# Cross attention and a mixture of experts on one core: contexts of batches 0 and 1 projected first, empty rows stored expert by expert, a last tile in chunks, a plan in pieces

## The chip, the cores and the metric

The kernel runs on one core of one Trainium2 chip. All data are float32. A core has a matrix engine (TensorE, PE in the profile, with its weight loads PEld), VectorE (DVE), ScalarE (ACT), GpSimd (POOL), SyncE (SP, used here only to issue transfers) and 16 DMA engines. Each engine runs its own list of instructions in order and waits for the others by semaphores. The metric is the device time in microseconds (us) from start to end of one execution; smaller is better.

## The reference

`x` and `ctx` are 8 batches of 256 rows of 512 numbers. First attention: the rows of x, normalised, are queries in 32 heads of 16; the rows of the context are keys and values in 8 groups that 4 heads share. Then a mixture of experts: every row goes through a shared network (704 wide) and through two of eight experts (352 wide), chosen from two of four groups.

```python
h = layernorm(x)
score = einsum(h @ Wq.T, ctx @ Wk.T) / 4           # per head; keys of a group for 4 heads
x = x + softmax(score) @ (ctx @ Wv.T) @ Wfc.T + bfc
h = layernorm(x)
scores = softmax(h @ gate_weight.T)                 # 8 experts, 4 groups of 2
w, i = group_limited_topk(scores)                   # 2 groups, in them 2 experts
routed = sum_n w_n * (silu(h @ gate_n.T) * (h @ up_n.T)) @ down_n.T
shared = (silu(h @ sh_gate.T) * (h @ sh_up.T)) @ sh_down.T
return x + routed + shared
```

On the host, weights are only permuted.

## The kernel before, in words

**Attention** (`attention`, from line 539). A batch is 8 units; a unit is 8 (head, half of the queries) pairs, one PSUM tile of 128 x 2048 scores. The steps of a unit:

- `maxima` (L810, L819): 16 matmuls put the scores with queries on the partitions into the tile `s`; DVE reduces it to the row maxima `nm` (2.29 us).
- `place` (L827 to L833): the maxima are transposed and written into a 17th row of the queries `qT`, so that the next product subtracts them.
- `weights` (L843, L851): 8 matmuls of 17 x 512 give the transposed scores less their maxima, in the same PSUM region as `maxima`; ACT takes exponentials (`ex`, 1.88 us).
- `values` (L862) multiplies `ex` by the values, and `divide` scales.

There is one region of PSUM for scores (`ps_s`, 8 KB a partition). The maxima of a later unit and the exponentials of an earlier one alternate in it, so PE does other work in between: the queries, keys and values of later batches (`project`, L713 to L795), the output projection of an earlier batch (`close`, L890), its router (L942) and its shared expert (`Shared.pieces`, L172 to L203).

**The planner.** Each of these works is a generator that emits a few instructions and then yields `(cost, open, rest)`: the PE time just emitted, whether a PSUM tile is still open (others then do not cut in), and for how much PE work the next piece should be put off, because another engine has to finish first. Costs are estimates in us. `Others.fill(now, least, most, warm)` emits pieces between two steps of attention, choosing the work furthest behind its due time; where nothing is ready, it calls `warm()`, which is two 128 x 128 matmuls of the identity that nobody reads. `finish(s)` emits pieces until `s` is done. With this the order on PE, ACT, DVE and SP is fixed when the kernel is built. POOL's order is left to the framework, which places POOL's instructions itself.

**Norms.** `normed(b)` takes mean and variance of batch b's rows on DVE, the reciprocal deviation on POOL (`pow`, L682), and centres the rows on DVE (L686).

**Start of the program.** SP loads batch 0's rows and context (L642 to L647), then `wq`, then batch 1's rows and context; ACT issues `wkv`. After 8 `warm` calls come batch 0's norm, then `project(0)`: keys and values (L720, L731), their copies (L741, L742), transposed rows (`tx`, L694, copies `xT`), queries (`pq`, L776), and the transfer of the queries into bands (`qT`, L791). `put` moves the keys into bands by DMA (L749). `copy` goes to ACT or DVE as `copy.free` says.

**Transfers among the attention.** `transfers()` (L1203) is a generator that is advanced once per step of attention: `wfc`, `bfc`, the router's and the shared expert's weights, then zeros to the rows behind the experts' tables, then one transfer (L1216) that writes zeros to the first 128 rows of each of the eight experts' tables in `rows`: 2112 KB from an `empty` tile of 264 KB.

**Closing a batch.** `close(b)` loads the batch's rows of x again as residual (`acc`, 2 transfers of 256 KB on SP), POOL adds the bias (L894), PE makes 4 + 4 matmuls `fc` per half (L901), DVE adds (L910), and the second norm follows.

**Routing.** `router(b)` computes gates and positions; GpSimd scatters the normalised rows to `rows` (L1026). After the last batch `plan` (L1034 to L1120) computes on DVE which tile of 128 rows belongs to which expert, from counts: about 30 small operations of up to 0.85 us each. Its yields have `rest` 0 and are "free", so the planner emits them one after another. The last batch's shared expert is left over and runs beside what follows; its products `act` (L185, L186) are DVE's too.

**Experts** (`routed`, L341 to L536). 35 tiles of up to 128 rows run: 8 first ones (one per expert), 24 full ones, 3 that two experts share. Per tile: load `xs` (L377), turn it (`rx`, `rxT`, L388 to L390), 8 matmuls of 128 x 352 for gate and up (`rg`, L421), silu on ACT (L429), product on DVE (`ract`, L431), three transposes (`ra`, `raT`, L437 to L440), 3 (or 6, with two experts' halves) matmuls `ro` (L449), scaling by the routing weight on DVE (`ry`, L457), and an indirect transfer by POOL that adds the rows to the result in memory (`y<-ry`, L460). The order of a step is: turn the next tile, `up` of this one, `down` of the one before, `turn_act` of this one. The added rows of one tile wait for those of the tile before, since both may write the same row. All weights `wgu_all`, `wd_all` stay in SBUF and are loaded on SP, the first ones while attention ends. A second run under a condition (L525) was not executed.

Of the kernel before, what the change touches and what calls it, by code (L numbers as in the profile page):

```python
# [340 lines left out]
def routed(ctx, tc, ps_m, wgu, wd, ident, rows, t_exp, t_row, t_one, t_all, t_end, blank, out, tail, right):  # L341
# [69 lines left out]

    def up(i):
        e = exps[i] = i if i < N_EXP else value(t_exp, i - N_EXP, ENG.PE, N_EXP - 1)
        gu = [ps_g.tile([P, F], F32, tag=f"g{k}", name=f"rg{i}_{k}") for k in range(2)]
        xT = xTs.pop(i)
        for k in range(2):
            for c in range(NC):
                f = slice(k * F, (k + 1) * F)
                w = wgu_all[:, bass.ds(e, 1), c, f].rearrange("p o f -> p (o f)")
                for part, w in halves(i, w, wgu_2[:, c, f]):  # L420
                    nc.tensor.matmul(  # L421
                        gu[k][part],
                        lhsT=xT[:, c, part],
                        rhs=w,
                        start=(c == 0),
                        stop=(c == NC - 1),
                    )
        sg = work.tile([P, F], F32, tag="sg", name=f"rsg{i}")
        nc.scalar.activation(sg, gu[0], AF.Silu)  # L429
        acts[i] = work.tile([P, F], F32, tag="act", name=f"ract{i}")  # L430
        nc.vector.tensor_mul(acts[i], gu[1], sg)  # L431
# [10 lines left out]
    def down(i):  # L442
        e = exps.pop(i)
        o = ps_y.tile([P, D], F32, tag="y", name=f"ro{i}")
        aT = aTs.pop(i)
        for fc, (_, fn) in enumerate(FCH):
            w = wd_all[:fn, bass.ds(e, 1), fc].rearrange("p o d -> p (o d)")
            for part, w in halves(i, w, wd_2[:fn, fc]):
                nc.tensor.matmul(  # L449
                    o[part],  # L450
                    lhsT=aT[:fn, fc, part],
                    rhs=w,
                    start=(fc == 0),
                    stop=(fc == len(FCH) - 1),
                )
        y = work.tile([P, D], F32, tag="y", bufs=3, name=f"ry{i}")
        nc.vector.tensor_scalar(y, o, w1s.pop(i), None, ALU.mult)  # L457

        for to, (part, _) in zip(ids.pop(i), halves(i, None, None)):
            nc.gpsimd.indirect_dma_start(  # L460
                out=out,
                out_offset=bass.IndirectOffsetOnAxis(ap=to, axis=0),
                in_=y[part],
                in_offset=None,
                compute_op=ALU.add,
            )

# [28 lines left out]
    def run(tiles):  # L496
# [3 lines left out]
        for n, i in enumerate([*tiles, None]):  # L500
            if 3 <= n + 2 < len(tiles):
                load(tiles[n + 2])
            if i is not None and i + 3 < N_EXP:
                up_weights(i + 3)
                down_weights(i + 3)
            for k, at in zip(halfs, seconds):
                if at == n:
                    second(tiles[k])
            if n + 1 < len(tiles):
                turn(tiles[n + 1])  # L510
            if i is not None:
                up(i)
            if n > 0:
                down(tiles[n - 1])
            if i is not None:
                turn_act(i)
# [22 lines left out]
def attention(  # L539
# [102 lines left out]
    def load_batch(b):  # L642

        xt = load_tiles(None if b == 1 else p2, b, "x", 1)
        cT = p2.tile([P, NC, S], F32, tag="cT", name=f"cT{b}")
        nc.sync.dma_start(cT, ctxT[b])
        return xt, cT  # L647

    loaded = {0: load_batch(0)}
    wkv_sb = cp.tile([P, NC, 2 * KVH * HD], F32, name="wkv_sb")  # L650
    nc.scalar.dma_start(wkv_sb, wkv)
    wq_sb = cp.tile([P, NC, D], F32, name="wq_sb")
    nc.sync.dma_start(wq_sb, wq)
    loaded[1] = load_batch(1)
# [45 lines left out]
    def normed(b):  # L700

        yield 0, False, 3.0 if b > 2 else 0, True
        xt, _ = loaded[b]
# [9 lines left out]
    def project(b):  # L713

        xt, cT = loaded.pop(b)
# [3 lines left out]
        for c in range(NC):  # L719
# [7 lines left out]
            if c % 2:  # L727
                yield 0.88, True, 0
        for kc in range(QC):
# [8 lines left out]
            if kc == 0:  # L738
                yield 0.88, True, 0
        k = p1.tile([P, S], F32, tag="k", name=f"k{b}")  # L740
# [5 lines left out]
        def put(G, dma):  # L746
# [4 lines left out]
        put(0, nc.sync)  # L751
        if b > 0:
            put(1, nc.sync)
        yield 0.88, False, 0

        xT = p1.tile([P, NC, S], F32, tag="xT", name=f"xT{b}")
# [3 lines left out]
        if b == 0:  # L760
            put(1, nc.scalar)

        nxt = b + 1 if b > 0 else 2
        if nxt < B and nxt not in loaded and b != 1:
            loaded[nxt] = load_batch(nxt)
# [268 lines left out]
    def plan():  # L1034
# [4 lines left out]
        yield 0, False, 0, True  # L1039
# [24 lines left out]
        yield 0, False, 0, True  # L1064
# [17 lines left out]
        yield 0, False, 0, True  # L1082
# [6 lines left out]
        for name, sl, start, end, base in (  # L1089
# [13 lines left out]
            yield 0, False, 0, True  # L1103
            nc.vector.tensor_mul(here, one, base.unsqueeze(1).to_broadcast(shape))
            nc.vector.tensor_reduce(row[:, sl], here, AX.X, ALU.add)

# [15 lines left out]
    PROJECT = 12 * 0.88 + 2 * 0.44  # L1122
    CLOSE = 2 * (0.44 + 4 * 0.88)
# [20 lines left out]
    for _ in range(8):  # L1144
        warm()
# [7 lines left out]
    projected = [others.add(project(0), PROJECT, 0, 1, norms[0])]  # L1153
    others.finish(projected[0])
    gates = {}
    for b in range(1, B):
        start = -LAG if b < DEEP else UNITS * b - 5.5 * LAG
        projected.append(
            others.add(project(b), PROJECT, start, UNITS * b - 1.5 * LAG, projected[-1], norms[b])
# [43 lines left out]
    def transfers():  # L1203
# [10 lines left out]
        yield  # L1214

        nc.sync.dma_start(  # L1216
            rows[: N_EXP * S_R].rearrange("(e s) w -> s e w", s=S_R)[:P],
            empty.unsqueeze(1).to_broadcast([P, N_EXP, W]),
        )

    loads = transfers()
    others.fill(-LAG, 2.0, 2.0, warm)
# [104 lines left out]
```

## Time and profile before

Three runs took 961.0, 955.32 and 957.47 us, median 957.47. The profiled execution itself took 959.21; its span is 957.4.

| stage | from to (us) | length | PE busy | DVE busy | clock |
|---|---|---|---|---|---|
| loading | 0 to 5 | 5.0 | 3.2 | 1.2 | 1.00 |
| attention, batch 0 | 5 to 100 | 95.0 | 93.0 | 48.8 | 1.00 |
| closing of batch 0 | 100 to 121 | 21.0 | 17.8 | 15.5 | 0.84 |
| attention up to batch 3's shared expert | 121 to 480 | 359.0 | 355.1 | 221.9 | 1.00 |
| the rest of attention | 480 to 620 | 140.0 | 139.8 | 76.2 | 1.00 |
| last router, plan | 620 to 655 | 35.0 | 33.1 | 18.8 | 1.00 |
| experts | 655 to 930 | 275.0 | 274.3 | 69.6 | 1.00 |
| last tile and end | 930 to 957.4 | 27.4 | 10.4 | 3.5 | 0.75 |

"Busy" is the time in which an engine has an instruction under way; length less busy is idle. The clock is the share of full speed that was granted to TensorE. The profile also tells, for every wait, which engine and instruction ended it; it follows the chain of work from the last instruction back; and it counts transfers by queue. Arrows such as `nm<-s` mean output from input; `x16` counts instructions.

### The profile page before, as it was taken

What the parts mean: (1) busy time and instruction counts of PE and PEld (TensorE: products, weight loads), DVE (VectorE), ACT (ScalarE), POOL (GpSimd) and SP (SyncE); (2) the same over time, 40 slices, a digit from 0 to 9 for tenths busy, and PEclk for the clock granted to TensorE, in tenths of its full rate; (3) what the DMA queues carried; (4) which work ended last, traced back from release to release, by engine and by line L of the source; (5) the groups of instructions that cost most, each with busy time, mean ns of one, the idle gap of its engine ahead of it and who ended that gap; (6) DMA issues with size and microseconds to landing.
All of it is one profiled execution on the core that took longest, in us unless ns stands there. A gap on an engine that the chain in (4) does not pass through costs nothing.

```text
span 957.4 us, 12926 instructions
## 1 busy us (share of the span) xinstructions
PE 926.7 (97%) x4989; PEld 545.7 (57%) x4989; DVE 455.5 (48%) x1026; ACT 202.9 (21%) x256; POOL 134.0 (14%) x171
## 2 busy tenths in 40 slices
PE   8999899999999999999999999999999999999992
PEld 8765466455545554664654645675666565565661
DVE  3653756656666755654775645361222222222221
ACT  1223033223223222222232231101111111111110
POOL 4000100211101101010121021120111121211211
PEclk9999899999999999999999999999999999999997
DMA  6368310120111111011111011089953443533322
GB/s 219 92 176 275 93 51 2 58 55 29 46 56 34 47 22 47 5 48 35 34 47 45 1 47 45 32 303 371 398 118 67 108 120 67 152 75 64 55 32 32
DMA packets 37790, 86.22 MB, mean 90 GB/s; under 512 B 6176, under 2 KB 14624, under 8 KB 35808
## 3 DMA queue, kind: packets, MB, share of 16 engines
q1 hardware_dynamic: 29040, 66.43, 21.5%
q0 software_dynamic: 7648, 17.83, 8.8%
q10 hardware_dynamic: 1040, 1.12, 0.4%
q8 instruction: 42, 0.69, 0.3%
q14 instruction: 20, 0.16, 0.1%
HBM read 54.99 MB, written 25.93 MB: 85 GB/s over the span
## 4 chain that ended last, share of the span: by engine, by line
PE 84%; DMA 4%; DVE 4%; SPq 3%; issue 1%; ACT 1%; POOL 1%; ACTq 0%; POOLq 0%; DVEq 0%
PE rg L421 17%; PE gu L172 14%; PE ro L449 9%; PE o L192 9%; PE s L843 6%; PE s L810 6%; PE fc L901 5%; PE av L862 5%; PE pq L776 4%; PE rx L388 2%; DMA rows<-empty 1%; DVE nm L819 1%; PE ra L437 1%; SPq L749 1%; SPq L791 1%
## 5 line engine op out<-in xcount | busy, mean ns | idle before, releaser
L819 DVE TENSOR_REDUCE nm<-s 128x8 f32<-128x2048 f32 x64 | 146.5, 2288 | 75.4 <-PE s L810 73.2
L421 PE MATMUL rg<-wgu_all,rxT 128*128 (+2 forms) x560 | 171.6, 459 | 0.0
L172 PE MATMUL gu<-hT,gu_w 128*128 128x256 f32 x704 | 167.1, 386 | 2.6 <-DVE act L186 1.9
L851 ACT ACTIVATE ex<-s 128x2048 f32<-128x2048 f32 x64 | 120.2, 1878 | 226.6 <-PE s L843 215.1
L172 PEld LDWEIGHTS gu<-hT,gu_w 128*128 128x128 f32 x704 | 128.9, 190 | 43.9 <-issue 24.1
L421 PEld LDWEIGHTS rg<-wgu_all,rxT 128*128 128x128 f32 (+1 forms) x560 | 101.1, 186 | 54.3 <-issue 6.9
L449 PE MATMUL ro<-wd_all,raT 128*128 (+5 forms) x210 | 96.5, 595 | 0.8 <-DVE raT L439 0.8
L460 POOL DMA_INDIRECT y<-ry,rid x38 | 58.4, 1537 | 254.5 <-DVE ry L457 197.5
L192 PE MATMUL o<-down,act 128*128 128x512 f32 x192 | 90.1, 604 | 0.3 <-DVE q L333 0.3
L431 DVE TENSOR_TENSOR ract<-rg,rsg 128x352 f32<-128x352 f32 x35 | 18.4, 525 | 141.1 <-PE rg L421 141.1
L810 PE MATMUL s<-kT,qT 16*128 16x256 f32 x1024 | 75.0, 404 | 3.5 <-DVE nm L819 3.3
L843 PE MATMUL s<-qT,kT 17*128 17x512 f32 x512 | 73.0, 640 | 2.9 <-DVE nm L819 2.2
L810 PEld LDWEIGHTS s<-kT,qT 16*128 16x128 f32 x1024 | 47.3, 186 | 34.4 <-ACT ex L851 14.9
L449 PEld LDWEIGHTS ro<-wd_all,raT 128*128 128x128 f32 (+3 forms) x210 | 38.4, 186 | 44.2 <-issue 37.1
L901 PE MATMUL fc<-wfc_sb,o 128*128 128x512 f32 x128 | 61.9, 610 | 0.1
L776 PE MATMUL pq<-xT,wq_sb 128*128 128x256 f32 x256 | 60.9, 385 | 0.8 <-ACT xT L333 0.8
L862 PE MATMUL av<-ex,v 128*32 128x512 f32 x512 | 61.5, 598 | 0.0
L1026 POOL DMA_INDIRECT rows<-lnf,idx x32 | 31.7, 991 | 209.5 <-DVE idx L1020 147.8
L457 DVE TENSOR_SCALAR ry<-ro,rw 128x512 f32<-128x512 f32 x35 | 26.3, 751 | 71.2 <-PE ro L449 71.2
L390 ACT COPY rxT<-rx 128x512 f32<-128x512 f32 x35 | 20.5, 586 | 185.0 <-PE rx L388 185.0
L192 PEld LDWEIGHTS o<-down,act 128*128 128x128 f32 x192 | 34.0, 190 | 41.5 <-issue 40.3
L776 PEld LDWEIGHTS pq<-xT,wq_sb 128*128 128x128 f32 x256 | 46.8, 190 | 14.1 <-issue 7.3
(176 smaller groups left out, 719.8 us busy)
## 6 DMA issues: line engine op xcount, KB each, us to landing
wgu_all<-wgu SPq DMA_DIRECT2D x8, 1408.0 KB
xs<-rows SPq DMA_DIRECT2D x32, 264.0 KB
wd_all<-wd SPq DMA_DIRECT2D x8, 768.0 KB
wgu<-wgu SPq DMA_DIRECT2D x3, 1408.0 KB
cT<-ctxT SPq DMA_DIRECT2D x8, 512.0 KB
acc<-x SPq DMA_DIRECT2D x16, 256.0 KB
y<-acc SPq DMA_DIRECT2D x16, 256.0 KB
x<-x SPq DMA_DIRECT2D x14, 256.0 KB
```

Of the source, the lines that this page charges most:

```text
L172: nc.tensor.matmul(ps[:, i], lhsT=self.gu[k][:, c, i * P : (i + 1) * P], rhs=hT[:, c], start=(c == 0), stop=(c == NC - 1),)
L192: nc.tensor.matmul(ps, lhsT=act[:, k, q * P : (q + 1) * P], rhs=self.down[:, k], start=(i == 0), stop=(i == len(SCH) - 1),)
L421: nc.tensor.matmul(gu[k][part], lhsT=xT[:, c, part], rhs=w, start=(c == 0), stop=(c == NC - 1),)
L449: nc.tensor.matmul(o[part], lhsT=aT[:fn, fc, part], rhs=w, start=(fc == 0), stop=(fc == len(FCH) - 1),)
L460: nc.gpsimd.indirect_dma_start(out=out, out_offset=bass.IndirectOffsetOnAxis(ap=to, axis=0), in_=y[part], in_offset=None, compute_op=ALU.add,)
L776: nc.tensor.matmul(ps[:, i], lhsT=wq_sb[:, c, part], rhs=xT[:, c], start=(c == 0), stop=(c == NC - 1),)
L810: nc.tensor.matmul(ps[:, r, j], lhsT=qT[band, G, j0 + j, qc * P : (qc + 1) * P], rhs=kT[band, G], start=True, stop=True,)
L819: nc.vector.tensor_reduce(nms[b, G, j0][:, qc], ps, AX.X, ALU.max, negate=True)
L843: nc.tensor.matmul(ps[:, r], lhsT=kT[band, G, kc * P : (kc + 1) * P], rhs=qT[band, G, j0 : j0 + 2], start=True, stop=True,)
L851: nc.scalar.activation(ex, ps, AF.Exp, scale=HD**-0.5)
L862: nc.tensor.matmul(av[32 * r : 32 * r + 32], lhsT=vs[b % DEEP][:, kc, 4 * G + r], rhs=ex[:, r], start=(kc == 0), stop=(kc == QC - 1),)
L901: nc.tensor.matmul(ps, lhsT=o[:, c, qc * P : (qc + 1) * P], rhs=wfc_sb[:, c], start=(c == 0), stop=(c == NC - 1),)
```

## The change

It has four parts.

1. **Contexts first.** A batch's load is divided in `load_context` and `load_rows`. SP now issues: context 0, rows 0, context 1, `wq`, rows 1. `project` gives its key and value part to a new generator `keys(b)`. At the start there are 5 `warm` calls instead of 8 (there are 17 in the whole program before and after); then `keys(0)`, the first norm, the first two pieces of `keys(1)`, and only then the rest of `project(0)`. The remainder of `keys(1)` is emitted where the planner wants it. For later batches `keys(b)` stands at the head of `project(b)`. Batch 1's copy of the keys gets another buffer, and the copies during the first `fill` go to DVE instead of ACT.
2. **Empty rows expert by expert.** The one transfer of 2112 KB becomes eight of 264 KB, one per step of attention.
3. **Plan in pieces.** The plan's yields ask for a `rest` of 1.7 instead of 0, and one yield is added, so that pieces of the last shared expert come between.
4. **Last tile in chunks.** `run` calls `last(i, before)` for the last tile: gate product, silu, `down` of the tile before, and then the up product in three chunks of 128, 128 and 96 columns, each followed by its product on DVE, its transpose and its `down` matmuls as soon as they can go. The matmuls of other tiles are the same, in new functions `product`, `down_chunk`, `add_up`.

Since the planner decides from costs and rests, parts 1 to 3 also shift the order of other pieces. On PE the order between batch 0 and 480 us differs by small swaps; from batch 3's shared expert to the last tile it is the same. On SP, the `acc` loads of batch 0 stand behind the query transfers of batch 4 in the new order; before they stood ahead of six pieces of them. On POOL, batch 5's deviation stands ahead of batch 0's bias adds in the new order, and behind them before.

```diff
+    def last(i, before):
+        of_expert(i)
+        g = ps_g.tile([P, F], F32, tag="g0", name=f"rg{i}_0")
+        product(g, i, slice(0, F))
+        sg = work.tile([P, F], F32, tag="sg", name=f"rsg{i}")
+        nc.scalar.activation(sg, g, AF.Silu)
+        down(before)
...
+        def values_of(fc):
+            f0, fn = FCH[fc]
+            u = ps_g.tile([P, F], F32, tag=f"g{int(fc < 2)}", name=f"ru{i}_{fc}")[:, :fn]
+            product(u, i, slice(F + f0, F + f0 + fn))
+            nc.vector.tensor_mul(a[:, f0 : f0 + fn], u, sg[:, f0 : f0 + fn])
+
+        def turned(fc):
+            f0, fn = FCH[fc]
+            ps = ps_m.tile([P, P], F32, tag="m", name=f"ra{i}_{fc}")
+            nc.tensor.transpose(ps[:fn], a[:, f0 : f0 + fn], ident)
+            nc.vector.tensor_copy(aTs[i][:fn, fc], ps[:fn])
+
+        values_of(0)
+        values_of(1)
+        turned(0)
+        values_of(2)
+        turned(1)
+        down_chunk(o, i, 0, FCH[0][1])
+        turned(2)
+        for fc in (1, 2):
+            down_chunk(o, i, fc, FCH[fc][1])
+        del xTs[i]
+        add_up(o, i)
...
-    loaded = {0: load_batch(0)}
+    contexts = {0: load_context(0)}
     wkv_sb = cp.tile([P, NC, 2 * KVH * HD], F32, name="wkv_sb")
     nc.scalar.dma_start(wkv_sb, wkv)
+    loaded = {0: load_rows(0)}
+    contexts[1] = load_context(1)
     wq_sb = cp.tile([P, NC, D], F32, name="wq_sb")
     nc.sync.dma_start(wq_sb, wq)
-    loaded[1] = load_batch(1)
+    loaded[1] = load_rows(1)
...
+    def project(b):
+        if b > 1:
+            yield from keys(b)
+        xt = loaded.pop(b)
...
         nxt = b + 1 if b > 0 else 2
         if nxt < B and nxt not in loaded and b != 1:
-            loaded[nxt] = load_batch(nxt)
+            contexts[nxt] = load_context(nxt)
+            loaded[nxt] = load_rows(nxt)
...
-        yield 0, False, 0, True
+        yield 0, False, 1.7, True
...
-    for _ in range(8):
+    for _ in range(5):
         warm()
...
-    projected = [others.add(project(0), PROJECT, 0, 1, norms[0])]
+    others.finish(others.add(keys(0), PROJECT_KEYS, 0, 1))
+    others.finish(norms[0])
+    of_keys = others.add(keys(1), PROJECT_KEYS, 0, 1)
+    for _ in range(2):
+        others.step(of_keys)
+    projected = [others.add(project(0), PROJECT - PROJECT_KEYS, 0, 1, norms[0])]
     others.finish(projected[0])
...
-        yield
-
-        nc.sync.dma_start(
-            rows[: N_EXP * S_R].rearrange("(e s) w -> s e w", s=S_R)[:P],
-            empty.unsqueeze(1).to_broadcast([P, N_EXP, W]),
-        )
+
+        for e in range(N_EXP):
+            yield
+            nc.sync.dma_start(rows[e * S_R : e * S_R + P, :], empty)
 
     loads = transfers()
+    copy.free = "DVE"
     others.fill(-LAG, 2.0, 2.0, warm)
```

## The prediction

> **What bounds the kernel now.** First the page: busy time and the granted clock by slices.
>
> ```profile
> PE 926.7 (97%) x4989; PEld 545.7 (57%) x4989; DVE 455.5 (48%) x1026; ACT 202.9 (21%) x256; POOL 134.0 (14%) x171
> PEclk9999899999999999999999999999999999999997
> ```
>
> TensorE (PE) carries the program. Both kernels issue the same matmuls, 17 `warm` calls included, apart from the split of one tile. So I count the time as PE work plus PE's idle time plus what a lowered clock costs, and ask which idle goes and which comes. Second view: stages, cut where the clock changes (columns: stretch, length, busy of PE, PEld, DVE, ACT and POOL, clock, DMA share, GB/s).
>
> ```profile
> 5.00:114.00 109.00, 103.98 (x711) 72.34 (x710) 60.29 (x86) 24.60 (x30) 11.02 (x23) 1.00 0.60 179
> 114.22:121.05 6.83, 6.83 (x27) 4.34 (x28) 3.93 (x5) 0.36 (x1) 0.57 (x1) 0.50 0.00 1
> 121.05:620.00 498.95, 494.89 (x3038) 275.78 (x3037) 298.06 (x608) 136.34 (x147) 53.11 (x79) 1.00 0.12 37
> 620.00:655.00 35.00, 33.09 (x128) 23.20 (x127) 18.84 (x86) 2.88 (x7) 6.78 (x7) 1.00 0.83 315
> 930.00:957.40 27.40, 10.43 (x31) 5.24 (x29) 3.47 (x8) 0.46 (x1) 4.65 (x3) 0.75 0.24 30
> ```
>
> Idle of PE: 5.02 us up to 114, 4.06 in 499 us of attention, 1.91 in the stage of the last router and the plan, 17 at the end. In the second row the clock is halved for 6.83 us, which costs 6.83 x 0.5 = 3.41. Third, who PE waited for (total, times, longest):
>
> ```profile
> PE s L810 <- DVE nm L819: 3.3, 2, 3.1
> PE gu L172 <- DVE act L186: 1.9, 1, 1.9
> PE ro L449 <- DVE raT L439: 0.8, 1, 0.8
> PE pq L776 <- ACT xT L333: 0.8, 1, 0.8
> PE s L843 <- ACT ex L851: 0.6, 1, 0.6
> ```
>
> Fourth, the chain of waits through the longest of these, and at the end (start, length, what).
>
> ```profile
> 100.34 5.45 DMA acc<-x
> 105.85 1.26 POOL acc L894
> 107.47 1.26 POOL acc L894
> 108.73 0.67 POOL rstda L682
> 109.43 1.00 DVE x L686 x2
> 111.97 2.19 DVE nm L819
> 114.20 2.09 PE s L810 x16
> ...
> 937.29 0.76 DVE ry L457
> 938.32 4.97 DMA y<-ry,rid
> ```
>
> Batch 0's residual rows arrive late, POOL adds the bias in its order, batch 5's norm stands behind it on POOL, and VectorE (DVE), in order, holds the row maxima of a score tile until 109.43. PE idles 3.11 us and then runs at half clock. At the end the last scatter waits until the one before has landed.
>
> **Part 1, contexts first.** The counts are unchanged; three `warm` calls move from the start into the attention. One call is 4 recorded matmuls, at full clock 2.15 / 19 = 0.113 us each (the timeline of the `warm` tile after 5.0 us), so 1.36 us leave and return; interleaved pairs of calls in the timeline take 1.06 to 1.20 instead of 0.90, so the return may cost 0.2 more. I take 0. Idle that can go: 0.14 before the first key matmul (7.30), 0.84 before the queries (12.76), and the first score group, 1.81 us instead of the 1.08 of the next, held by the query transfer (0.73): 1.71. Now x, key weights and context (1.5 MB) are in front of the first matmul; afterwards 1 MB. At the 436 GB/s of 5.0 to 7.2 us that is 1.2 us sooner, so keys start near 6.0; five `warm` calls end at 1.81 + 16 x 0.212 + 4 x 0.113 = 5.7. Keys 3.6, half of batch 1's keys 1.8, transposes 0.9 and 1.0 more of batch 1 fill PE until 13.3, when the copies of x (two of 0.60) are just done. New: the second score group waits for DVE, which now first copies batch 1's keys, values and x (0.42 + 0.41 + 2 x 0.65) and centres batch 2's x (1.0): about 0.4 idle. Sum -1.3; bounds -1.7 and, if the query transfer lands as late as it did relative to its copies, 0.
>
> **Part 2, empty rows expert by expert, and the order around batch 0's close.** Before, one 2112 KB store is issued at 77.51; the chain follows it for 14.26 us, the eight query issues behind it take 9.55 us against 5.60 for another eight, and SyncE (SP) reaches the residual loads at 100.34. Afterwards a 264 KB store is issued at a time, and in the new POOL order batch 5's norm stands ahead of the bias adds. That unties DVE from them. But SP's new order puts the residual loads behind the eight query transfers of batch 4 and one chunk: about 98.9 (queries copied) + 8 x 0.64 + 0.6 = 104.6 on my count of PE, later than before. Queued behind them: a chunk, batch 5's key bands, batch 6's loads, first needed 10 us on. The first load took 5.45 us with 1 MB of other loads ahead; with one chunk (14.26 / 8 = 1.8 us) and small pieces ahead I take 4: landing 108.7, bias add done 110.0. DVE wants it after the maxima of the fourth group, near 110.4. So no wait, with 0.4 to spare. The statistics of batch 5's x before the second group's maxima cost PE 0.9. Idle 3.11 becomes 0.9 and the halved clock (3.41) goes: -5.6. The 0.61 at 87.8 and 0.18 at 99.2 are gone in the new order by the same count, exponentials being 1.88 and the work between them over 2: -0.7. Bounds: -7.3 (no idle left), and from the other side the load 5.8 us later in SP's order (nine issues of 0.64), all of it PE idle beyond the old 3.11: +5.8.
>
> Here a rule of the skill speaks against the change. The Trainium skill, "DMA: Bandwidth & Descriptors", section Bandwidth / Measured, says to batch transfers to at least 1 MiB, and gives about 2.0 us fixed plus bytes at 436 GB/s for each (section Anatomy of one DMA). An estimate by that page: a chunk in front costs 2.6 us instead of 1.8, the residual is 0.4 late, and the total below is 11.1 instead of 11.5. No row of this profile has such a chunk.
>
> **The stretch between, 121 to 480.** PE's order differs by small swaps, and is the same from batch 3's shared part on. The 4.06 us of idle there are 0.6 at most each. I take 0; bounds -2 and +6.5, the price of one more 3.1 us stall with its clock.
>
> **Part 3, plan in pieces.** Before, the plan is one block on DVE, 627.46 to 636.22, and the shared part's two products of 0.42 behind it hold PSUM: 1.91 us. In the new DVE order two products follow each piece. The first pieces end at 629.0, and the products of chunk 0 at 629.8; PE wants that bank at 635.2. The price: `hereh` ends three product pairs later (0.85 each, less one counted after it): 634.8 becomes 636.3, and SP, which holds the first `wd_all`, the first token tiles and two experts' weights until then, issues them 1.4 later (634.90 before). The first token tile is transposed at 649.22, then 647.3: 10 us after its issue, and the tables of tiles, done near 638.6, are read far later. Covered; if that cover of 10 us went, each late us would be PE idle. -1.9, bounds -1.9 and 0.
>
> **Part 4, last tile.** Gate product 8 x 0.296 from 929.77, then the down product of the tile before, 6 x 0.43: done 934.72 instead of 937.27, so its scatter starts at 935.8 instead of 938.32, lands 4.97 later at 940.7, and POOL can start the last one 0.75 later (as 943.29 to 944.04): 941.5. PE: three chunks of up, 8 matmuls each at 0.122 (1.95 / 16, the 128-wide value group), three transposes of 0.11, 6 x 0.43: 940.6; scaling 0.75 and 0.27: 941.6. The old 0.84 wait for the copies goes, since each copy (0.28) has a product beside it. 944.04 - 941.6 = -2.4. Bounds: -2.5, and 0 if landing took as much longer. What follows the last scatter (13.4 us) moves along.
>
> **Sum.** -1.3 - 5.6 - 0.7 + 0 - 1.9 - 2.4 = -11.9; less the 0.4 that moved warms and extra switches may cost, -11.5. The profiled execution took 959.21 (span 957.4 and 1.8 around it): 947.7. It stands 1.7 over the median 957.47, inside the runs' 955.32 to 961.0, whose mean is 957.9; I place the median at 947.
>
> **Rivals.**
> - *The stall stays.* The residual load takes 6.6 us, as the second one did before, and lands at 111.2: add done 112.5, 2.1 us late, PE idles 3.0 and the clock halves again. For it: the loads moved back in SP's order. Against: nothing large is ahead. 2.1 + 3.4 on top of 947: 952.5.
> - *A new stall in batches 1 to 3.* DVE's order of norms, maxima and products differs there, and 3.1 us of idle was enough to lower the clock. For it: DVE is 60% busy, in order. Against: 0.6 is the longest wait now. One such stall, 6.5: 953.5.
> - *The front gains nothing.* The empty rows were not the reason, only POOL's order, and something else is as late; parts 3 and 4 alone: 957.5 - 4.3 = 953.2, or 955 with the moved warms and a later `wd_all`.
> - *Slower than before.* One mechanism: batch 0's residual loads, now the last of a queue of eight query pieces and a chunk, land so late that DVE stands still. PE's idle then grows by each late us plus 3.4 for the clock. It eats 11.5 from 8.1 us late on, a landing after 117, 12 us after the issue: 958 and more, 962 at 12 us late. For it: the eight issues behind the old bulk store did take 4 us longer. Against: no load of the profile took that long.
>
> **How the numbers follow.** Forecast, 943 to 951: 0.56. Stall stays: 0.17. New stall: 0.12. Front gains nothing: 0.08. Slower: 0.07. The first, with the two stalls in full or half, gives 943 to 955 (the new stall and the lost front end there); outside are the slower case and some 0.1 of the others. About 0.5% (4.8 us, so 952.7 and 962.3) is what a measurement can tell from no change. Faster: the forecast, two thirds of the first rival and a part of the next two, 0.73; same: the rest and half of the slower case, 0.21; slower 0.06.
>
> **What would show it.** The granted clock stays 1.0 from 5 us to the last tile; no wait of PE for the maxima over 1.5 us; the first key matmul near 6.0; no wait of the shared part for `act`; the last two scatters about 5.7 apart at 935.8 and 941.6, less the 9 us won earlier. The forecast is wrong if a row of half clock stands near 105 to 115, if POOL's bias add starts after 111, or if PE waits for a `wgu` or token load after 640.

## The result

The changed kernel takes 947.54 us (median of 6 runs, 946.71 to 948.08); the kernel before took 959.2 beside it (955.32 to 963.95). The ratio is 0.9876, with a 95% interval of 0.9847 to 0.9905. The profiled execution of the changed kernel took 946.92 us (span 945.1), that of before 959.21 (span 957.4): 12.3 us less in both measures.

The page of the changed kernel, busy time and granted clock by slices:

```profile
PE 922.8 (98%) x5005; PEld 545.0 (58%) x5005; DVE 454.2 (48%) x1028; ACT 202.6 (21%) x257; POOL 134.1 (14%) x171
PEclk9999999999999999999999999999999999999997
```

The slice with an 8 in the clock is gone. PE has 3.9 us less busy time; 3.41 of it is what the halved clock added before. The stages (stretch, length, busy of PE, PEld, DVE, ACT, POOL, clock, DMA share, GB/s), cut where the prediction cut them, the later ones some 8 to 12 us earlier:

```profile
6.01:114.00 107.99, 106.87 (x743) 75.11 (x741) 62.53 (x88) 25.09 (x32) 9.98 (x21) 1.00 0.59 173
114.00:121.05 7.05, 7.00 (x49) 5.03 (x52) 3.87 (x9) 1.88 (x1) 1.04 (x5) 1.00 0.69 219
121.05:612.00 490.95, 487.26 (x2987) 269.48 (x2980) 294.31 (x603) 134.13 (x146) 52.82 (x74) 1.00 0.11 35
612.00:645.00 33.00, 33.00 (x131) 23.52 (x129) 19.05 (x86) 2.88 (x7) 6.76 (x7) 1.00 0.80 312
918.00:945.10 27.10, 12.20 (x54) 7.29 (x52) 4.30 (x11) 0.46 (x1) 4.65 (x3) 0.80 0.25 31
```

The first row has 1.1 us of idle where 5.0 stood, the second has a full clock, the stage of the plan has no idle at all. The waits of PE (total, times, longest):

```profile
PE s L909 <- DVE nm L885: 1.9, 3, 0.8
PE s L876 <- ACT ex L917: 0.8, 2, 0.5
PE ra L443 <- DVE ract L437: 0.7, 1, 0.7
PE s L876 <- DVE nm L885: 0.6, 1, 0.6
PE pq L842 <- DVE acc L201: 0.3, 1, 0.3
```

The maxima (L876, which was L810) waited 0.6 us for DVE instead of 3.3, and the wait of `gu` for `act` is gone. POOL around the close of batch 0 (start, length, what, idle before and who ended it):

```profile
100.35 0.69 POOL L735 TENSOR_TENSOR rstda<-rstda,mhalf 128x2 f32<-128x2 f32 x1 [23.37 <-DVE rstda L734]
108.92 2.50 POOL L960 TENSOR_TENSOR acc<-acc,bfc_sb 128x512 f32<-128x512 f32 x2 [7.88 <-DMA acc<-x]
```

Batch 5's deviation is computed 8 us ahead of the bias adds that it had stood behind. The residual rows still come late: they land at 108.9 (the semaphore of their transfer then tells that the data are in place), 3.1 us later than the 105.8 of the kernel before. Nobody on PE waits for them. SP's issues, before (start, time to issue them all, what, number):

```profile
77.51 0.59 SPq L1216 DMA_DIRECT2D rows<-empty  x1
82.82 9.55 SPq L791 DMA_DIRECT2D qT<-q  x8
100.34 0.90 SPq L638 DMA_DIRECT2D acc<-x  x2
102.87 5.77 SPq L791 DMA_DIRECT2D qT<-q  x8
```

and after:

```profile
98.59 5.13 SPq L857 DMA_DIRECT2D qT<-q  x8
103.76 0.58 SPq L1298 DMA_DIRECT2D rows<-empty  x1
104.39 0.93 SPq L686 DMA_DIRECT2D acc<-x  x2
```

So before, all eight query transfers of batch 4 stood behind the residual loads `acc`, not six of them. The end of the chain of waits:

```profile
922.06 2.58 PE ro L451 x6
924.64 0.91 PE ru L420 x8
...
926.13 4.88 DMA y<-ry,rid
931.01 0.02 issue
```

Stage by stage, the two profiled executions compare as follows. Idle is every gap of PE over 0.06 us; the last tile is measured from the first expert product to the last scatter (655.25 to 944.04, and 645.00 to 931.76). The -1.3 that was predicted for the start is divided here: -1.0 of idle before the queries, +0.4 of a new wait behind them, -0.7 of a first score group that takes less of PE's own time.

| stage | before | after | difference | predicted |
|---|---|---|---|---|
| idle up to the queries | 0.98 | 0.00 | -1.0 | -1.0 |
| idle from there to 121 | 4.20 | 0.95 | -3.2 | -2.5 |
| lost to half clock, 114 to 121 | 3.41 | 0 | -3.4 | -3.4 |
| idle, rest of attention | 3.98 | 3.61 | -0.4 | 0 |
| idle at the plan | 1.91 | 0 | -1.9 | -1.9 |
| last tile | 288.79 | 286.76 | -2.0 | -2.4 |
| the rest (PE's own time) | | | -0.4 | -0.3 |
| sum (span) | 957.4 | 945.1 | -12.3 | -11.5 |

### The profile page after: what moved, and what is told of

The parts are those of the page before. It is cut to its first block, busy times and chain, and to the rows that moved or that the text cites. A ratio compares the mean times of both kernels' runs of the same rounds, so it can differ in the third digit from the quotient of the medians.

```text
span 945.1 us, 12978 instructions
## 1 busy us (share of the span) xinstructions
PE 922.8 (98%) x5005; PEld 545.0 (58%) x5005; DVE 454.2 (48%) x1028; ACT 202.6 (21%) x257; POOL 134.1 (14%) x171
## 4 chain that ended last, share of the span: by engine, by line
PE 93%; DVE 3%; ACT 1%; DMA 1%; issue 0%; POOL 0%; ACTq 0%; POOLq 0%; DVEq 0%
PE rg L420 17%; PE gu L172 16%; PE ro L451 9%; PE o L192 9%; PE s L909 7%; PE s L876 7%; PE fc L967 6%; PE pq L842 6%; PE av L928 6%; PE rx L388 2%; PE pkv L786 1%; DVE nm L885 1%; PE pkv L775 1%; PE ra L443 1%; PE tn L893 1%; PE warm L1198 1%
## 5 line engine op out<-in xcount | busy, mean ns | idle before, releaser
L420 PE MATMUL rg<-wgu_all,rxT 128*128 (+2 forms) x552 | 169.2, 459 | 0.0
L876 PE MATMUL s<-kT,qT 16*128 16x256 f32 x1024 | 73.4, 400 | 1.5 <-ACT ex L917 0.8
L876 PEld LDWEIGHTS s<-kT,qT 16*128 16x128 f32 x1024 | 46.3, 184 | 30.9 <-ACT ex L917 14.1
```

Source lines behind the costliest of these rows:

```text
L420: nc.tensor.matmul(dst[part], lhsT=xTs[i][:, c, part], rhs=w, start=(c == 0), stop=(c == NC - 1),)
L876: nc.tensor.matmul(ps[:, r, j], lhsT=qT[band, G, j0 + j, qc * P : (qc + 1) * P], rhs=kT[band, G], start=True, stop=True,)
```

## The experiments

Two theories stood against each other for the largest term, the close of batch 0. STORE: the bulk store of empty rows holds up the queries' transfers, and through SP's order the residual rows. ORDER: what matters is that POOL has batch 5's deviation ahead of the bias adds. The diffs are against the kernel before where nothing else is said. The kernel before was run again beside them. Its median was 957.75 us (34 runs) beside the store, the contexts, the plan and the last tile alone; 957.64 (17 runs) beside the store in one piece, the first try at a late residual, the filling and the eight warm calls; 957.48 (19 runs) beside the remaining three. Against these 70 runs the 947.54 of the changed kernel, measured at another time, is a gain of about 10 us, not the 11.7 of the first comparison.

### The store alone

```diff
         nc.sync.dma_start(blank, empty[:R])
-        yield
-        nc.sync.dma_start(
-            rows[: N_EXP * S_R].rearrange("(e s) w -> s e w", s=S_R)[:P],
-            empty.unsqueeze(1).to_broadcast([P, N_EXP, W]),
-        )
+        for e in range(N_EXP):
+            yield
+            nc.sync.dma_start(rows[e * S_R : e * S_R + P, :], empty)
```

> The kernel before, and of the change only this: the one 2112 KB store of empty rows becomes eight stores of 264 KB, one per step of attention. The order on PE is the one of before, and so is POOL's: batch 0's bias adds stand ahead of batch 5's deviation. Theory STORE (the bulk store holds up the query transfers behind it, and through SyncE's order the residual loads): the eight query issues take about 5.6 us instead of 9.55, the residual loads are issued near 96 instead of 100.3, POOL's bias adds are done before 104, PE's idle of 3.11 us before the maxima and the half clock of 6.83 us are gone; 3.11 + 3.41 + some 0.7 of shorter waits: 7 us less than before, about 952. Theory ORDER (what mattered is that POOL has the deviation ahead of the bias adds): the stall stays, within 1 us of before, about 959.

Measured: 953.65 us, ratio 0.9958 (0.994 to 0.9975), 4.1 us less; STORE's 7 us were counted from the profiled 959.2. The timelines of SP and POOL in its profile, around the close of batch 0:

```profile
84.78 5.16 SPq L791 DMA_DIRECT2D qT<-q  x8
98.72 0.92 SPq L638 DMA_DIRECT2D acc<-x  x2
```

```profile
103.92 2.49 POOL L894 TENSOR_TENSOR acc<-acc,bfc_sb 128x512 f32<-128x512 f32 x2 [21.70 <-DMA acc<-x]
107.65 0.70 POOL L682 TENSOR_TENSOR rstda<-rstda,mhalf 128x2 f32<-128x2 f32 x1 [1.24 <-DVE rstda L681]
```

The eight query issues took 5.2 us, the residual loads were issued at 98.7 (not 96), and the deviation, still behind the bias adds, now waits 1.24 us for DVE and not for them. PE's idle there is 0.46. In this execution the context of batch 4 came 1.47 us late and the clock was halved once for that, at 81.5. So cutting up the store is enough to end the stall in the old order: the residuals land at 103.9, 1.9 us earlier than in the kernel before.

### The contexts alone

The edit is part 1 of the change, with the bulk store left in one piece.

> The kernel before, and of the change only the first part: contexts of batches 0 and 1 ahead, 5 warm calls, keys of batch 1 early. The empty rows are still one store of 2112 KB. The order on PE is that of the changed kernel up to the last tile but for the plan's pieces, and POOL has batch 5's deviation ahead of batch 0's bias adds. Theory ORDER: the stall and the half clock are gone although the store is in one piece; start 1.0, close of batch 0 6.0, short waits 0.7: about 951.5. Theory STORE: the query transfers behind the store still take 9.5 us and the residual loads come late; the bias adds start after 111, PE waits for the maxima for 2 us or more and the clock halves: 957 or more.

Measured: 951.7 us (950.22 to 954.96), ratio 0.9946 (0.9926 to 0.9966), 6.05 us less. POOL's timeline in its profile:

```profile
100.97 0.69 POOL L687 TENSOR_TENSOR rstda<-rstda,mhalf 128x2 f32<-128x2 f32 x1 [24.77 <-DVE rstda L686]
106.81 2.50 POOL L912 TENSOR_TENSOR acc<-acc,bfc_sb 128x512 f32<-128x512 f32 x2 [5.15 <-DMA acc<-x]
```

The number is ORDER's. In the new order the store is issued at 84.6, behind the queries of batch 3 and not ahead of them. The residuals land at 106.7, later than the 105.8 of the kernel before, and yet no wait of PE over 0.5 us follows up to 200 us. So the new order is enough too, and not by bringing the residuals earlier: in this order PE has no need of them yet. The order changes on SP, POOL, DVE and PE at once; no run changes POOL's alone, so what each queue's order gives is not separated. The runs spread over 4.7 us: some still lost time that the profiled one doesn't show.

### Both, without plan and last tile

> The kernel before, and of the change the first two parts: contexts first and empty rows in eight stores; not the plan, not the last tile. With rows_only and contexts_only it fills the square of store and order. If either of the two alone removes the main stall and the other only trims what is left, the two together are little better than contexts_only (951.7): 950.5 to 951.5, with the narrow spread of the changed kernel. If they add up (4.1 and 6.0 less than 957.7): 947.6. The parts left out, plan and last tile, are then worth this time less 947.5: 2.0 + 1.5 to 2.0 by the traces, 3.5 to 4.

Measured: 950.82 us (949.9 to 951.34), ratio 0.9927 (0.9899 to 0.9955). The two parts don't add up (4.1 and 6.05, together 6.7 by the medians): either one removes the stall, and the second mainly narrows the spread, from 3.0 or 4.7 us in 12 or 11 runs to 1.4 in 6. Against the 947.54 of the changed kernel, which was measured at another time, plan and last tile together are worth 3.3 us, a little under the 3.5 expected.

### The changed kernel with the store in one piece

```diff
-        for e in range(N_EXP):
-            yield
-            nc.sync.dma_start(rows[e * S_R : e * S_R + P, :], empty)
+        yield
+        nc.sync.dma_start(
+            rows[: N_EXP * S_R].rearrange("(e s) w -> s e w", s=S_R)[:P],
+            empty.unsqueeze(1).to_broadcast([P, N_EXP, W]),
+        )
```

> The changed kernel with its empty rows in one store of 2112 KB again, everything else as changed. The orders on PE and POOL are those of the changed kernel. Theory ORDER: the store does no harm any more, within 0.7 us of the changed kernel, about 947.5. Theory STORE: the residual loads come late again, 3 to 6 us more than the changed kernel, 951 to 954, with a wait of PE for the maxima near 110.

Measured: 948.43 us, but over 946.53 to 951.94 in 6 runs, where the changed kernel lies within 946.71 to 948.08. The profiled execution has no long wait, and its span is 945.2. Once the order is new, the chunks change the typical run by less than these few runs can tell; two of the six were 3 us and more above the changed kernel, and what they waited for was not in a profile.

### A late residual, first try

```diff
-        for e in range(N_EXP):
+        for _ in range(3):
             yield
-            nc.sync.dma_start(rows[e * S_R : e * S_R + P, :], empty)
+        yield
+
+        nc.sync.dma_start(
+            rows[: N_EXP * S_R].rearrange("(e s) w -> s e w", s=S_R)[:P],
+            empty.unsqueeze(1).to_broadcast([P, N_EXP, W]),
+        )
```

> The changed kernel, but the eight stores of empty rows are one store of 2112 KB, issued directly ahead of the residual loads of batch 0. It tests the prediction's rival of a slower kernel: residuals that land late cost each late us and 3.4 us for the clock. The store took 14.3 us in the trace of before; issued at 103.8, the residuals land near 118 to 119 instead of 108.9 (1.5 us of which were slack), so PE stands 7 to 9 us and the clock halves: 10 to 12 us more than the changed kernel, 957 to 960. Rival (the loads pass the store on other engines' queues, or the planner's other work covers it): under 3 us more, below 951.

Measured: 947.57 us, as the changed kernel. The expectation missed because the edit was one step short: the store was issued at 91.3, ahead of batch 4's query transfers, 13 us before the residual loads at 104.1, and these landed at 107.0. It tells nothing about a late residual; it shows that the store costs nothing in this earlier place.

### A late residual, second try

The same with one more `yield`, so that the store stands directly ahead of the residual loads.

> The changed kernel, but the eight stores of empty rows are one store of 2112 KB that stands directly ahead of batch 0's residual loads on SyncE, behind the queries of batch 4 (one step later than in the run late_rows, where the store was issued at 91.3 and its residuals landed at 107.0, 15.8 us after it). Issued at 103.8, the residuals land near 119 to 120, the bias adds are done 1.3 and 2.5 us later, DVE wants the first at 110.2. Prediction's rival (a late residual stops DVE, and through it PE): PE waits 9 to 11 us for the maxima or the exponentials behind them, and the clock is halved for two stretches of 3.41 us after it: 12 to 14 us more than the changed kernel, 959 to 962. Other theory (DVE has other work to go on with, or the loads pass the store): under 4 us more.

Measured: 954.46 us (952.73 to 955.45), 6.9 more than the changed kernel. The chain of waits shows each link of the prediction's slower rival:

```profile
105.46 0.59 SPq L1299
106.05 0.04 issue
106.09 9.63 DMA acc<-x
...
115.86 1.27 POOL acc L960
117.13 0.02 issue
117.15 0.70 DVE acc L976
...
118.71 2.27 DVE nm L885
120.98 0.04 issue
121.02 2.09 PE s L909 x8
```

PE idled 4.98 us, and the clock was halved for 6.83 us, partly while PE still stood (columns as in the stages above):

```profile
119.45:126.28 6.83, 5.26 (x23) 3.76 (x24) 5.08 (x9) 1.88 (x1) 1.04 (x5) 0.50 0.28 96
```

PE worked 5.26 us at half clock, which cost 2.6; with the idle that is 7.6, where this profiled execution took 8.1 more than that of the changed kernel and the median 6.9. The mechanism is as expected, the size is not: the loads landed 10.3 us after the issue of the store, not 15.8. By the semaphores in the trace the store landed at 115.08 and the first load at 115.72, so the load did wait for all of it; but the store took 9.6 us from issue to landing. In the three other kernels that issue it whole and later than the kernel before (contexts alone, store in one piece, first try) it took 9.3 to 10.1. The 14.26 of the kernel before began with about 6 us in which no packet of the store moved, behind a 1536 KB load issued at 74.73, and the 15.8 of the first try held 12.8 us in which the loads were not yet issued. Against the changed kernel the landing is 6.9 us later, for 5.0 us of idle: 1.9 us of lateness cost nothing.

### Filling the idle

Against the kernel before, directly ahead of the stalled maxima (the twelfth):

```diff
             copy.free = "ACT"
+            if i == 20:
+                full = ps_m.tile([P, NC, P], F32, tag="m", name="filler")
+                for c in range(11):
+                    nc.tensor.matmul(full[:, c % 4], lhsT=ident, rhs=ident, start=True, stop=True)
             maxima(k)
```

> The kernel before with 11 matmuls of the identity (22 recorded ones, 2.5 us) into a tile that nobody reads, put into PE's order directly ahead of the maxima that waited 3.11 us. The wait itself stays; only PE's idle in it is filled. If the half clock that followed is the price of the idle: the granted clock stays 1.0 through 105 to 125, and the time falls by 3.4 us at an unchanged start of those maxima (114.2): about 955.8. If the clock falls for another reason, or the filling delays what follows: no gain or up to 2.5 us more, 959 to 962. If the spread of the kernel before (955 to 964) comes from this clock, it shrinks to that of the changed kernel (1.4 us).

Measured: 957.34 us (955.31 to 963.33) beside 957.64, ratio 0.9999 (0.9981 to 1.0018): no gain, and the spread stays. The timeline of PE in its profile shows the filling at work:

```profile
111.85 2.62 PE L1233 MATMUL filler<-ident 128*128 128x128 f32 x22
114.99 1.15 PE L810 MATMUL s<-kT,qT 16*128 16x256 f32 x16 [0.53 <-DVE nm L819]
```

The clock held 1.00 there (1.15 us for the maxima where it had been 2.09), as it should if the idle was what lowered it. But in the same execution the clock was halved later, at the plan, after a wait of 1.92 (stages, columns as above):

```profile
632.38:635.79 3.41, 1.49 (x7) 1.02 (x6) 3.13 (x15) 0.38 (x1) 0.00 (x0) 1.00 0.68 226
635.79:639.20 3.41, 3.41 (x10) 2.71 (x9) 0.39 (x1) 0.00 (x0) 0.00 (x0) 0.50 1.04 398
```

Over all timed runs the mean granted clock was 0.9924 with the filling and 0.9911 in the 17 runs of before beside it: 0.0013 of 957 us, 1.2 us of clock kept. The filling takes 2.5 us also where the residual comes early, which could eat this; that was not measured apart. So the link from idle to clock is shown at this place, in one execution, and that filling pays is not.

### Plan alone, last tile alone

The edits are parts 3 and 4 of the change, each by itself on the kernel before.

> The kernel before, and of the change only the plan in pieces. The prediction's theory: PE's wait of 1.91 us for the product act near 635 goes, nothing else changes: first turn of an expert's tile 1.9 us earlier (647.3), 957.3 against 959.2. Rival: the tables or the second weights come later by 1.4 us and PE waits for them after 640: no gain, 959.

> The kernel before, and of the change only the last tile in chunks. By the trace of the changed kernel: 2.0 us less (957.2), the last three scatters 5.7 us apart, each starting 0.75 us after the landing of the one before. Rival (the scatter of the tile before waits only for its own scaled rows, as in the prediction): it starts at 935.8 and the last one at 941.5 in the time of before, 2.4 less.

Measured: the plan 954.87 us (952.06 to 960.16), ratio 0.9973 (0.9954 to 0.9992); the last tile 955.38 (953.65 to 959.85), ratio 0.9991 (0.9975 to 1.0008), so it can't be told from before by the runs. Both still carry the stall at the close of batch 0, whose size differs from execution to execution. The stalled wait of PE, and POOL's bias adds on its timeline, in the profile of the plan alone:

```profile
PE s L810 <- DVE nm L819: 5.7, 1, 5.7
```

```profile
110.05 2.49 POOL L894 TENSOR_TENSOR acc<-acc,bfc_sb 128x512 f32<-128x512 f32 x2 [28.30 <-DMA acc<-x]
```

and the same two of the last tile alone:

```profile
PE s L858 <- DVE nm L867: 1.7, 1, 1.7
```

```profile
104.93 2.62 POOL L942 TENSOR_TENSOR acc<-acc,bfc_sb 128x512 f32<-128x512 f32 x2 [23.62 <-DMA acc<-x]
```

These two and the kernel before have the same order of work up to 480 us. The maxima start 5.5 us after the end of the second bias add in all of them (108.73 to 114.20, 112.53 to 118.00, 107.56 to 113.03), so the landing of the residual alone sets the wait: 3.1, 5.7 or 1.7 us, with the clock halved in the first two and not in the third.

The parts' own terms are read from stages. From batch 7's first exponential group to the first expert tile's turn it is 120.8 us before (528.46 to 649.22), 118.6 with the plan in pieces, 118.6 in the changed kernel: -2.2. From the first expert product to the last scatter it is 288.8 before, 287.3 with the new last tile alone, 286.8 in the changed kernel. The difference of 0.5 is the landing of one scatter, 5.35 us in the one and 4.88 in the other.

### Warm calls

```diff
-    for _ in range(5):
+    for _ in range(8):
         warm()
```

on the changed kernel, and, to leave out the 12 calls among the attention,

```diff
-        dull = warm if i < 44 else None
+        dull = None
```

> The changed kernel with 8 warm calls at its start instead of 5, and so 20 in all. The keys' matmuls started at 6.13 in the changed kernel, directly after the warm calls. If the start is set by the warm calls, three more delay it by 3 x 4 x 0.113 = 1.4 us (more where the clock is still halved), 949. If it is set by the first context's arrival near 6, or the earlier full clock gives it back: under 0.5 us more, 947.5 to 948.

> The changed kernel without the 12 warm calls among the attention (the 5 at the start stay); since a call counts as work for the planner, some pieces of batches 0 to 3 change places. It asks what the three calls that the change moved into the attention cost. If the calls stand in waits that PE would have anyway (for the copies of transposed rows, for row maxima), the time is the same within 1 us or grows where an idle window halves the clock, 946.5 to 950. If they are work on top: 12 x 0.45 = 5.4 us less, 942.

Measured: eight warm calls 949.42 us, 1.9 more than the changed kernel; the first key matmul starts at 7.06 instead of 6.13. In both profiles it follows the warm calls without idle, so they set the start there. With the contexts alone and with the store in one piece the five calls end at 5.7, and the key matmul starts at 6.08, after 0.4 us of waiting for the key weights. The start explains 0.9 of the 1.9 us; 0.7 more is one wait of PE at 78.0 in this profile that the changed kernel does not have; its cause stays open. Without the fillers 950.48 us (949.21 to 954.3), 2.9 more: PE idles 12.0 us instead of 5.3, and its clock falls. Two stages of its profile, columns as above:

```profile
62.29:65.70 3.41, 1.73 (x12) 0.73 (x12) 2.67 (x6) 2.51 (x3) 0.00 (x0) 1.00 0.57 94
65.70:72.52 6.82, 6.81 (x27) 5.09 (x28) 2.29 (x1) 0.00 (x0) 0.00 (x0) 0.50 0.46 110
```

The calls mostly stand in waits that would be there anyway. This kernel also changes places of pieces of batches 0 to 3, and POOL's bias adds are back ahead of the deviation, so the 2.9 is not the price of the calls alone.

## Why the prediction was right

The sum was 947.7 for the profiled execution and 947 for the median; measured are 946.92 and 947.54.

**Start.** The first key matmul was predicted near 6.0 and stands at 6.13, partly by luck: the forecast had it wait for the loads, with the five calls done at 5.7, and in this execution the calls end at 6.3, all of them at half clock, since the full clock came only at 6.01. The idle fell by the 1.0 taken, the first score group takes 1.15 us instead of 1.87, as taken too, and the new wait of 0.4 did not come: 1.7 in all where 1.3 was taken. The profiled execution of before was a lucky one here: with eight warm calls and the old loads the first key matmul stands at 7.30, 7.67, 8.10, 7.78 and 8.30 in five profiles, with five calls and contexts first at 6.08 to 6.24 in seven. PE's clock reaches full speed at another time in each (5.0 to 7.7 in the former).

**Close of batch 0.** The steps came out one by one: residual loads issued at 104.39 (104.6 predicted), landed at 108.9 (108.7), first bias add done at 110.19 (110.0), 0.63 us of idle for the statistics of batch 5's x (0.9), a full clock. DVE did wait 0.26 us for the bias add instead of having 0.4 to spare; PE had other work and did not notice. That the landing is right to 0.2 us is partly luck: the load was taken as 4 us, an estimate, and took 4.5, and its issue came 0.2 sooner. Two things the prediction did not say. It priced a stall as if it were one size; it is 1.7 to 5.7 us in three executions of the same order, and the profiled one lay in the middle. And it told the story as one cause: the stall needs both the bulk store and the old order, and changing either one ends it, the store by bringing the residuals earlier, the order by letting them be late. That holds up to a point: 6.9 us later still, in the second try, PE stalls again in the new order.

In the prediction a rule of the skill spoke against the chunks. The Trainium skill, "DMA: Bandwidth & Descriptors", section Anatomy of one DMA, whose fit is for transfers that GpSimd issues, gave an estimate of 2.6 us for a chunk. By the semaphores in the trace the chunk ahead of the residual loads, issued by SP at 103.76, landed at 106.46, 2.70 us, and the one issued at 90.53 landed at 92.98, 2.45 us: as a time from issue to landing the estimate is good. But the load behind a chunk loses less. The residual took 4.5 us from issue to landing in the changed kernel and in the one with the first two parts, where a chunk is issued just ahead, and 2.9 in the three kernels whose store is whole and issued 13 us or more earlier (contexts alone, store in one piece, first try): 1.6 us, nearer to the 1.8 that the prediction took. That 1.8 was still partly luck, since it is an eighth of the 14.26 us that held other loads. One sentence there is wrong: the kernel before does have a chunk of 264 KB, issued at 75.67; it landed at 85.66, behind that same load of 1536 KB. The section Bandwidth / Measured, on batching to 1 MiB, did not decide: the kernel with nothing but smaller stores is 4.1 us faster, because here what stands behind a store counts, not its rate.

**The stretch between.** Taken as 0, measured -0.4 of idle. No new stall appeared.

**Plan.** -1.9 predicted and measured (-2.2 over the longer stretch above, other gaps included). The later `hereh` and `wd_all` were covered, as argued: the first expert tile's turn moved by the whole gain. (The plan's 39 small operations take 0.41 us at most; 0.85 is a pair of products of the shared expert.) What was not counted is that the wait of 1.9 us can halve the clock (the filled kernel shows it), so that in some executions the plan in pieces saves 1.7 more.

**Last tile.** -2.4 predicted, -2.0 measured. The step that is off is "its scatter starts at 935.8": it was worked out from the scaled rows alone. But the scatter before had landed only at 935.60 in the trace of before, and POOL starts the next one 0.75 later, as the prediction itself used for the last scatter: 936.36. In the changed kernel it is 926.13, which is 936.38 with the 10.25 us won earlier. With it the last scatter comes at 942.0 instead of 941.6. The last three scatters of the changed kernel:

```profile
920.43 1.55 POOL L465 DMA_INDIRECT y<-ry,rid  x1 [6.53 <-DVE ry L462]
926.13 1.55 POOL L465 DMA_INDIRECT y<-ry,rid  x1 [4.15 <-DVE ract L496]
931.76 1.55 POOL L465 DMA_INDIRECT y<-ry,rid  x1 [4.08 <-DVEq L580]
```

The profile puts the middle one down to DVE's `ract`. But the scatter before it landed at 925.38, 0.75 us earlier, and in all seven profiles with the new last tile that scatter starts 0.75 us after the landing before it. So three scatters in a row now bound the end, not PE: they start 5.7 and 5.6 us apart.

**Rivals.** The slower kernel needed a landing after 117; in the run that made the residual late on purpose it was 115.7, and the time grew by 6.9 us. So the rival's mechanism is real, but its price is too high: each late us (7.0 from the 108.7 of the forecast) plus 3.4 for the clock would be 10.4. 1.9 us of the lateness cost nothing, and the halved clock cost 2.6, because PE stood for part of it. And what it lacked was a cause, since the one chunk ahead costs the residual 1.6 us. The stall that stays and the front that gains nothing are ruled out by the first two rows of stages. The new stall did not come.

## What to carry to other kernels

Follow a stall back link by link, with each queue's order in the new program beside it: where the links were dated from the trace, the answer here was good to 0.2 us, with some luck in the one link that was estimated. Look at the spread of the times as well as at the median: the kernel before varied by 9 us, and in it one wait that hung on the landing of one transfer was 1.7 us in one execution and 5.7 with a halved clock in another; the changed one varies by 1.4. Where a serial chain of transfers stands at the end, check each link against the landing of the one before, not only against its own data.

## What the runs showed of the hardware

The granted clock changes on a grid. In all profiles a stretch of one clock that begins and ends within the program is a multiple of 3.41 us: 109.23 (32 of them) until the stall in the kernel before, 6.83 halved, 75.09 (22) in the kernel with the store alone. The grid begins at another time in each execution, with the first full clock at 4.7 to 8.0 us.

How much idle lowers the clock was not what I expected. Waits of 3.11, 4.98 and 5.74 us did, for two units of the grid each. But 1.47 us (store alone, at 80.1, 42% of its unit) and 1.92 us (filled, at 632.7, 56%) did too, for one unit, and without the fillers a unit with 1.7 us of idle in pieces (62.3 to 65.7, 49%) did for two. And 1.92 us with the last tile alone, at 631.2, did not, though it took 53% of one unit of the grid. So the share of idle in a unit doesn't decide by itself; what else counts stays open. The Trainium skill, "TensorE: Matmul & The Clock Gate", section Part 1: The HAM clock gate, gives a free-running window of 3413 ns, which agrees with the grid, and a lowered clock after at least one idle window, which does not agree with 1.47 us.

The clock also goes with much of the spread of the kernel before. Of its 70 runs beside the experiments, 14 had a mean granted clock of 0.993 or 0.994 and took 954.9 us on average, 44 had 0.989 to 0.991 and took 958.7; the other 12, at 0.992, took 957.6. One halved unit is 3.41 x 0.5 / 957 = 0.0018 of the mean clock, so the second group lost about two units in the middle of the program; how much of the 3.8 us is clock and how much the idle that came with it was not separated.
